# Zero multiplications ahead of 61 TensorE operations, in the operation's own PSUM bank

## The chip, the cores and the metric

The kernel runs on one core of a Trainium2 chip. The metric is the time of one execution on the device in microseconds (us); lower is better. Times of the kernel before are given as the median of three executions. Everything else is read from one further execution that the hardware profiler recorded.

The engines are named as in the profile: PE is TensorE (PEld its weight loads), DVE is VectorE, ACT is ScalarE, POOL is GpSimd, SP is the engine that only issues DMAs here.

## The reference, cut to what matters

One layer of a "metaformer" over `x` of shape (8, 128, 128, 96), batch × height × width × channels: a filter in the frequency domain whose weights depend on the input, then a two-layer MLP in emulated low precision, both with residuals.

```python
# B, H, W, C = 8, 128, 128, 96;  MED = 192
x_pre = soa(einsum('bhwc,mc->bhwm', layernorm(x), w1))      # soa(t) = scale * relu(t)**2 + bias
xf    = rfft2(x_pre)                                        # over height and width
r     = softmax(fc2 @ soa(fc1 @ [mean(x), mean(relu(sp_w x))]))   # 3 rates per image and channel
comb  = sum_s r[s] * resized_filter[s]                      # complex, 128 x 65 x 192
x     = x + w2 @ irfft2(xf * comb)

t = layernorm(x)                                            # per token, 96 channels
h = relu(q16(q16(q8(t) @ q8(W1)) + q8(b1)))                 # q8: fp8 e5m2, q16: fp16
x = x + q16(q16(q8(h) @ q8(W2)) + q8(b2))                   # hidden width 384
```

## The kernel before, in words

The Fourier transforms are matrix products with cosine and sine tables, so nearly all of the arithmetic is on PE. For each of the 8 images there are three streams of work, named by a letter and the image number.

- Stream `a` (`before`): 32 steps of four image columns. `scale` on DVE makes the normalised tile `zT` from `xT` and the broadcast reciprocal deviations `rB`; `project` on PE (L672) multiplies it by `W1S`, one PSUM bank for each half (`i0` is 0 or 2); `rectify` and `square` on ACT follow; `transform` on PE (L701) transforms along the height; `put` on ACT (L708) moves it out and `store_y` writes it to DRAM. After the last step the chain `rate_v0`, `rate_p0`, ... `rate_n` computes the softmax over the three filters: `p` steps on PE (L757, L765, L766, L780), `v` steps on DVE (L753, L774, L775), `rate_e` on ACT.
- Stream `s` (`spectrum`): 33 groups of four frequency rows. `along_w` on PE (L874) transforms along the width; `filters_of` (L887) makes the filters; `copy_sr` (ACT) and two `make` (DVE, L913) read the `along_w` banks; DVE and POOL multiply by the filter; every second group `mix_low` and `mix` (L971, L984, L995) multiply by `w2` and `invert` (L1011) transforms back along the height. `rate_n` must be done before the filters are weighed.
- Stream `c` (`after`): 32 steps. `last` (L1123) finishes the inverse transform, `residual` on DVE (L1131) reads it; `measure`, `rstd` and `quantise` normalise; `turn` (key `turn8`, L1156) transposes on PE and `turned` (L1166, DVE) reads it; `first` (L1170) makes three hidden blocks, `accumulated` (L1177, ACT) and `biased` (L1181, DVE) follow, `hidden` (L1185, ACT) makes the fp8 tile `h8`; `second` (L1192) multiplies by `W2q`; `put` (L1203, ACT), `bias` (DVE), `add_up` (L1210, POOL) and `store` end it.

Streams overlap: stream `s` of an image runs beside `a` of the next and `c` of the one before. The first part of the execution has stream `a` of image 0 alone, the last part stream `c` of image 7 alone.

The order is written out by hand. Every operation has a planned time (`STREAMS`, `O`, `OWN`); `in_order` sorts the operations by it, respecting their needs, and hands out six PSUM banks: an operation gets its banks when they come free in that order. The result is one fixed list, emitted in that order; at the end each engine's instructions are tied into that order, so every engine, PE included, works through its list strictly first to last. A bank is a tile of a pool with one buffer for each tag:

```python
def bank(name):
    t = ps.tile([128, 512], F32, name=name, tag=f"bank{free_banks.pop(0)}")
    return t
```

so the first write of an operation into its bank waits until the last reader of the bank's previous tile has finished. That reader is on ACT or DVE. `zeros` is a constant bf16 tile of 128 × 64 zeros that `mix_low` already multiplies by to clear its banks. Semaphores are placed by the framework.

## Time and profile before

| | |
|---|---|
| median of three executions | 2752.43 us (2752.04 to 2754.02) |
| profiled execution, span from first to last instruction | 2754.4 us |
| PE busy | 2567.8 us, 93% of the span, 25130 matmuls and as many weight loads |
| DVE, ACT, POOL busy | 83%, 81%, 77% |
| mean granted PE clock | 0.970 of full speed |
| DMA | 618.05 MB, mean 224 GB/s |

The profiled execution's own time is its span; the page gives nothing around it. It is 0.07% above the median of the three. "Granted clock" is the share of its full clock that the throttle allowed PE at that time. A group's idle time is that of its engine just before its instructions, and the name behind the arrow is what ended the wait.

### The profile page before, as it was taken

Reading aid. Unit: us, or ns where it says so; the run is one execution under the profiler, and the core shown is the slowest. Engines: PE = TensorE matmul, PEld = TensorE weight load, DVE = VectorE, ACT = ScalarE, POOL = GpSimd, SP = SyncE. Lnnn points to the kernel's source line nnn. Section 1 sums busy time; section 2 is a strip of 40 time slices with the busy share of each in tenths; the row PEclk is TensorE's granted clock in tenths of the full one; section 3 lists DMA queues with packets and bytes.
Section 4 is the critical chain, followed back from the end, with each engine's and each line's share of the span. In section 5 each row is a group of like instructions: output and inputs, shape, how many; then the busy total and the mean of one; then the engine's idle time right before and its main releaser. Section 6 shows DMA issues by size and latency. Waiting matters only on the chain.

```text
span 2754.4 us, 69406 instructions
## 1 busy us (share of the span) xinstructions
PE 2567.8 (93%) x25130; PEld 1953.0 (71%) x25130; DVE 2276.1 (83%) x5887; ACT 2233.0 (81%) x4452; POOL 2122.2 (77%) x3246
## 2 busy tenths in 40 slices
PE   4989999999999999999999999999999998999765
PEld 2668877777677777777677777777777776677433
DVE  3557667798898999889898889889889878999786
ACT  2665556699888879889998878889988997888898
POOL 1239997888788878988688969888788886889432
PEclk9899999999999999999999999999999998999896
DMA  7888777977688866878687757888777774656441
GB/s 205 263 263 253 242 224 241 287 233 251 209 255 260 252 213 196 271 242 262 220 258 245 243 171 220 273 259 257 231 239 242 230 222 147 185 178 190 149 129 62
DMA packets 480023, 618.05 MB, mean 224 GB/s; under 512 B 174542, under 2 KB 381270, under 8 KB 479658
## 3 DMA queue, kind: packets, MB, share of 16 engines
q1 hardware_dynamic: 424386, 462.60, 56.8%
q10 hardware_dynamic: 55296, 151.02, 14.7%
q8 instruction: 199, 3.26, 0.5%
q14 instruction: 142, 1.16, 0.1%
HBM read 405.36 MB, written 208.16 MB: 223 GB/s over the span
## 4 chain that ended last, share of the span: by engine, by line
PE 68%; DVE 13%; ACT 7%; POOL 4%; DMA 4%; issue 3%; SPq 1%; POOLq 0%; ACTq 0%; DVEq 0%
PE px L672 13%; PE pz L874 10%; PE py L701 10%; PE pv L995 7%; PE pf L887 6%; PE pg L1011 5%; PE ph L1170 4%; PE pk L1123 4%; PE po L1192 3%; PE pv L984 3%; DVE t L916 3%; DVE y L1181 2%; ACT h L1185 2%; ACT y L1177 2%; DVE st L581 2%
## 5 line engine op out<-in xcount | busy, mean ns | idle before, releaser
L923 POOL TENSOR_TENSOR rr<-t,t 128x390 f32<-128x390 f32 x512 | 520.4, 1017 | 60.4 <-DVE t L916 60.0
L672 PE MATMUL px<-W1S,zT 97*128 97x240 f32 x2048 | 519.4, 379 | 34.1 <-DVE zT L659 29.2
L1177 ACT CAST y<-ph 128x512 f16<-128x512 f32 x768 | 456.0, 603 | 24.2 <-PE ph L1170 22.4
L672 PEld LDWEIGHTS px<-W1S,zT 97*128 97x128 f32 x2048 | 377.2, 194 | 130.0 <-issue 33.7
L1151 ACT ACTIVATE z<-t,ln_m,ln_r 128x96 fp8e5<-128x96 f32 x960 | 461.2, 492 | 8.6 <-POOL ln_m L614 5.7
L1181 DVE TENSOR_SCALAR y<-y,b1q 128x512 f16<-128x512 f16 x768 | 427.5, 568 | 28.2 <-ACT y L1177 25.6
L683 ACT ACTIVATE rl<-px 128x480 f32<-128x480 f32 x512 | 295.7, 581 | 177.5 <-PE px L672 160.2
L701 PE MATMUL py<-X,F 128*128 128x384 f32 x1024 | 430.7, 507 | 2.1 <-ACT X L690 1.9
L1185 ACT ACTIVATE h<-y 128x1536 fp8e5<-128x1536 f16 x256 | 386.2, 1509 | 2.2 <-DVE y L1181 1.6
L659 DVE SCALAR_TENSOR_TENSOR zT<-xT,rB 96x512 f32<-96x512 f32 x256 | 339.8, 1328 | 53.1 <-DMA rB<-Rd 26.5
L874 PEld LDWEIGHTS pz<-F,yt 128*128 128x128 f32 x2080 | 301.4, 192 | 72.0 <-DVE t L1131 5.9
L1210 POOL TENSOR_TENSOR t<-t,o 128x1536 f32<-128x1536 f32 x64 | 210.1, 3282 | 167.8 <-DVE o L1207 165.8
L874 PE MATMUL pz<-F,yt 128*128 128x130 f32 x2080 | 329.0, 281 | 10.2 <-DVE t L1131 4.7
L857 POOL TENSOR_TENSOR tb<-tb,r 128x384 f32<-128x384 f32 (+1 forms) x264 | 287.0, 1087 | 59.7 <-DVE r L808 23.1
L916 DVE TENSOR_TENSOR t<-dm,pf 128x390 f32<-128x390 f32 x512 | 282.6, 552 | 43.8 <-PE pf L887 18.4
L1170 PE MATMUL ph<-zT,W1q 96*128 96x512 fp8e5 x768 | 293.5, 397 | 19.1 <-DVE zT L1166 13.9
L708 ACT COPY yst<-py 128x384 f32<-128x384 f32 x512 | 246.4, 486 | 74.3 <-PE py L701 67.8
L916 DVE TENSOR_TENSOR t<-dp,pf 128x390 f32<-128x390 f32 x512 | 280.3, 548 | 0.0
L940 POOL TENSOR_TENSOR xf<-rr 128x378 f32<-128x378 f32 x256 | 255.3, 997 | 19.7
L995 PEld LDWEIGHTS pv<-w2A,xf 128*128 128x128 f32 x2048 | 246.8, 194 | 13.6 <-issue 1.5
L995 PE MATMUL pv<-w2A,xf 128*128 128x96 f32 x2048 | 255.2, 278 | 0.0
L938 POOL TENSOR_TENSOR xf<-rr 128x390 f32<-128x390 f32 x256 | 250.1, 977 | 0.0
(126 smaller groups left out, 5210.5 us busy)
## 6 DMA issues: line engine op xcount, KB each, us to landing
Yd<-yst ACTq DMA_DIRECT2D x256, 384.0 KB
yt<-Yd SPq DMA_DIRECT2D x256, 384.0 KB
xb<-in_x SPq DMA_DIRECT2D x64, 768.0 KB
xT<-in_xT SPq DMA_DIRECT2D x128, 384.0 KB
rB<-Rd SPq DMA_DIRECT2D x128, 384.0 KB
tb<-T SPq DMA_DIRECT2D x256, 192.0 KB
Vd<-gst ACTq DMA_DIRECT2D x128, 384.0 KB
xr<-in_x SPq DMA_DIRECT2D x64, 768.0 KB
```

The costliest lines, as they stand in the source:

```text
L659: nc.vector.scalar_tensor_tensor(zTs[(b * NU + u) % NZT][:C, :, :], kept["xT", hb][:, :, w].rearrange("c h w -> c w h"), 1.0, kept["rB", h ...
L672: nc.tensor.matmul(px[:, i * (MED + SCTX) : (i + 1) * (MED + SCTX)], lhsT=zTs[(b * NU + u) % NZT][:, i0 + i, :], rhs=W1S, start=True, stop ...
L701: nc.tensor.matmul(py, lhsT=F1, rhs=kept["X", u][:, i0 : i0 + 2, :].rearrange("h w m -> h (w m)"), start=True, stop=True)
L874: nc.tensor.matmul(pz[:, u * 2 * L : (u + 1) * 2 * L], lhsT=y, rhs=F2[:, cs, :], start=True, stop=True)
L916: nc.vector.tensor_tensor(work(name, g), kept[d, g], pair(g, sign, c), ALU.mult)
L923: nc.gpsimd.tensor_tensor(kept["rr", g][:, :, 2 * i : 2 * i + 2, :], kept[ta, g], kept[tb, g][:, :, ::-1, :], op)
L995: nc.tensor.matmul(kept["pv", p, r][:, i * C : (i + 1) * C], lhsT=kept["xf", g][:, cs, r, :], rhs=w2A, start=False, stop=(i == len(_column ...
L1151: nc.scalar.activation(z, t, AF.Identity, bias=m, scale=r, saturate=False)
L1170: nc.tensor.matmul(kept["ph", u, n], lhsT=W1q[:, n * 128 : (n + 1) * 128], rhs=kept["zT", u], start=True, stop=True)
L1177: nc.scalar.copy(kept["y", u][:, n, :], kept.pop(("ph", u, n)))
L1181: nc.vector.tensor_scalar(y, y, b1q[:, n : n + 1], 0.0, ALU.add, ALU.max)
L1185: nc.scalar.activation(kept["h8", u], kept["y", u], AF.Copy, saturate=False)
```

## The change

A table `WARM` lists, for 61 operations of PE, a number between 1 and 24; the numbers add up to 340. Before such an operation is emitted, `keep_warm` takes a tile in the first of the banks that the operation is about to use and emits that many matmuls into its first 64 partitions: `zeros` as weights (128 rows × 64 columns), and one column of `zeros` repeated 512 times as the moving operand. Each is a complete product of its own (`start` and `stop`), nobody reads it, and the operation then takes its own tile in the same bank. Nothing else is added, removed or moved: no DMA, no instruction of another engine, and the order of the old instructions is the same on every engine.

```diff
+WARM = {
+    ('a', 0): {('project', 0, 2): 24, ('project', 4, 2): 4, ('project', 6, 2): 6, ('project', 8, 2): 7, ('project', 16, 2): 9, ('project', 24, 2): 9, ('project', 28, 2): 5},
+    ('a', 1): {('transform', 1, 2): 4, ('project', 3, 0): 7, ('rate_p2',): 5},
+    ('a', 2): {('rate_p0',): 9},
+    ('a', 3): {('project', 3, 0): 4, ('rate_p2',): 10},
+    ('s', 3): {('along_w', 0, 0): 6},
+    ('c', 2): {('second', 19): 6, ('first', 21, 0): 5},
+    ('a', 5): {('rate_p2',): 9},
+    ('c', 3): {('second', 14): 3},
+    ('s', 4): {('mix_low', 12): 4},
+    ('a', 6): {('project', 0, 0): 5},
+    ('a', 7): {('project', 3, 0): 6, ('rate_p2',): 7},
+    ('s', 6): {('along_w', 0, 1): 2, ('invert', 13, 1): 22},
+    ('c', 5): {('turn8', 4, 3): 4, ('first', 24, 0): 5, ('first', 25, 0): 6},
+    ('s', 7): {('along_w', 9, 0): 3, ('along_w', 13, 1): 12, ('invert', 14, 0): 5},
+    ('c', 6): {('turn8', 6, 3): 2, ('second', 24): 2, ('first', 27, 0): 11, ('first', 29, 0): 8, ('first', 30, 0): 6},
+    ('c', 7): {('turn8', 0, 0): 16, ('first', 1, 0): 3, ('second', 1): 4, ('second', 2): 4, ('second', 3): 4, ('second', 4): 1, ('second', 5): 4, ('second', 6): 4, ('second', 7): 4, ('second', 8): 1, ('second', 9): 4, ('second', 10): 2, ('second', 13): 4, ('second', 15): 4, ('second', 16): 1, ('second', 17): 4, ('second', 19): 4, ('second', 20): 1, ('second', 21): 4, ('second', 23): 4, ('second', 24): 1, ('second', 25): 3, ('second', 26): 3, ('second', 27): 3, ('second', 30): 4, ('second', 31): 7},
+}
...
+    def keep_warm(op):
+
+        n = WARM.get(op.key[0], {}).get(op.key[1:], 0)
+        if n:
+            t = ps.tile([128, 512], F32, name="warm", tag=f"bank{free_banks[0]}")
+            for _ in range(n):
+                nc.tensor.matmul(t[:64, :], lhsT=zeros, rhs=zeros[:, :1].to_broadcast([128, 512]), start=True, stop=True)
...
     for op, banks in in_order(ops):
         free_banks[:] = banks
+        keep_warm(op)
         op.what(*op.args)
```

## The prediction

> **What bounds the kernel now.** I read the page first, then the chain of waits, [...] then the timeline at every place that the table names.

> ```profile
> span 2754.4 us, 69406 instructions
> ...
> PE 2567.8 (93%) x25130; PEld 1953.0 (71%) x25130; DVE 2276.1 (83%) x5887; ACT 2233.0 (81%) x4452; POOL 2122.2 (77%) x3246
> ...
> PE   4989999999999999999999999999999998999765
> ...
> PEclk9899999999999999999999999999999998999896
> ...
> PE 68%; DVE 13%; ACT 7%; POOL 4%; DMA 4%; issue 3%; SPq 1%; POOLq 0%; ACTq 0%; DVEq 0%
> ```

> PE is busy in nearly every slice from the third to the 33rd, and holds 68% of the chain. So a us of PE time saved or lost in the middle should mostly reach the end. In the last 150 us PE has idle time; there ACT is nearly full.

> The clock is not lost evenly. Stretches (start:end, length, then busy us and count of PE, PEld, DVE, ACT, POOL; then PE clock, DMA share, GB/s) [...]:

> ```profile
> 699.80:703.20 3.40, 1.55 (x17) 1.18 (x18) 3.37 (x12) 0.91 (x3) 3.32 (x5) 1.00 1.01 306
> 703.20:706.60 3.40, 3.40 (x9) 2.07 (x8) 1.03 (x2) 1.86 (x5) 3.15 (x8) 0.51 0.38 123
> ...
> 2645.40:2648.80 3.40, 2.24 (x18) 1.29 (x18) 3.02 (x8) 1.84 (x5) 3.23 (x6) 1.00 0.79 248
> 2648.80:2652.20 3.40, 1.38 (x17) 1.02 (x18) 2.81 (x10) 3.31 (x7) 1.59 (x8) 1.00 1.21 323
> 2280.20:2283.60 3.40, 1.47 (x39) 1.20 (x31) 3.30 (x13) 1.03 (x3) 3.31 (x6) 1.00 0.42 157
> 2283.60:2290.40 6.80, 6.80 (x36) 6.30 (x35) 4.01 (x10) 1.40 (x4) 2.73 (x5) 0.50 1.06 285
> ```

> [...] half-clock stretches are 3.4, 6.8 or 10.2 us, apart from the last. [...]

> **The price of one.** The nearest row is `first`, 512 moving columns with its own weight load.

> ```profile
> 2314.10 0.60 PE L1170 MATMUL ph<-zT,W1q 96*128 96x512 fp8e5 x2
> ...
> 2726.52 1.05 PE L1170 MATMUL ph<-zT,W1q 96*128 96x512 fp8e5 x2
> 2727.89 0.63 PE L1170 MATMUL ph<-zT,W1q 96*128 96x512 fp8e5 x1
> ```

> One takes 0.38 us at full clock (1035.74 in the timeline), two take 0.60: 0.22 us for each further one. At half clock 1.05 − 0.63 = 0.42. The 340 cost 340 × 0.22 = 75 us of PE time warm. Their weight loads lie beside the preceding product (a load of 128 columns of fp8 is about 0.10 us).

> **Where they cost nothing.** At 51 places the bank had been read out before PE went idle, and PE waited for an operand. There n × 0.22 is 0.4 to 0.8 of the wait, for instance:

> ```profile
> 701.65 0.25 PE L757 MATMUL pm<-ones,s 128*48 128x1 f32 x2 [2.59 <-DVE s L753]
> ...
> 2283.09 1.81 PE L780 MATMUL pl<-fc2T,hrep 36*128 36x192 f32 x6 [1.93 <-DVE hrep L775]
> ```

> 9 × 0.22 = 1.98 in 2.59 us, 7 × 0.22 = 1.54 in 1.93 us. They end 0.1 to 0.8 us before the operand comes, so the wait covers them. At half clock the cover is gone: 7 × 0.42 = 2.9. The framework could also make the operation wait for its last zero product to complete; one alone takes 0.38, so that is 0 to 0.16 us for each place, inside the same spare; I take 0.

> **Where they delay.** At ten places the wait was for the bank itself, so the zero products can begin only when the operation itself could, and everything behind it on PE's fixed list is later by all of them:

> ```profile
> 2301.84 0.55 DVE L913 TENSOR_TENSOR dm<-pz,sr 128x390 f32<-128x390 f32 x1
> ...
> 2302.53 1.62 PE L1011 MATMUL pg<-V,GL 128*128 128x384 f32 x2 [6.26 <-DVE dm L913]
> ```

> The 6.26 us before `invert 13` end when DVE's `make` has read the bank of `along_w 30`. Its 22 products then start at 2302.4 and take 22 × 0.22 = 4.8 us of full-speed PE time; behind them wait 30 us of PE work that is the chain itself. The ten, in us at full speed: `along_w` of s3 1.3, `mix_low 12` 0.9, `along_w` of s6 0.4, `invert 13` 4.8, `along_w 9` of s7 0.7, `along_w 13` of s7 2.6, `invert 14` 1.1: 11.8 on the chain. `turn8` of c5 (0.9) stands before PE's own 6 us of idleness, and the two of c6 (0.4 each) where ACT carries the chain: 0. Upper end, if the zeros run at half clock and don't raise it: 19.

> **What is gained.** What a half-clock stretch costs is half of the chain's PE time in it, since PE work doubles there:

> ```profile
> 2284.91 3.66 PE pv L995 x16
> ...
> 2311.94 1.81 PE pv L995 x16
> ```

> I added up the chain's PE pieces inside each half-clock stretch of the middle: from 423.4 us 6.8, 703.2 3.4, 1024.1 6.0, 1624.8 2.8, 1635.1 6.5, 1699.9 3.4, 2000.3 3.4, 2283.6 6.3; together 38.6. (In that from 1362.0 DVE has the chain: 0.) All but 1699.9 follow a wait that the table fills; filled, their windows come to 2.2 us busy and more. So (38.6 − 3.4)/2 = 17.6. PE then meets DVE (44 to 47 of each 50 us busy) sooner, so I let 85% through: 15.0; bounds 5 and 17.6.

> Stream a of image 0 has 22.9 us of the chain's PE time at half clock (78.6 to 85.4, 112.7 to 122.9, 181 to 184, 191 to 195), at most 11.4 to gain. But its chain alternates with DMAs (rB, xT, Yd), and a PE that arrives sooner waits longer for them, perhaps long enough to cool again. I take 45%: 5.1; bounds 0 and 11.4. The 24 before `project 0` gain nothing: from 30.5 they end by about 38, and the operand comes at 42.8, [...].

> The stops from 2297.3 and 2413.3 remain, as nothing can run before the bank is free. From 2566 on ACT or a POOL–ACT loop holds the chain. What is left to gain is `second 31`, 1.14 us cold against 0.68, and two small ones before it: 0.7; bounds −2 to +1 (its 7 products take 2.9 us cold in a wait of 1.95).

> **Sum.** −15.0 − 5.1 + 11.8 × 0.85 (10.0) − 0.7 = −10.8 us. Against the span of 2754.4 that is 2743.6. The median is 2.0 below that span, so 2741.6: **2742**.

> **Rivals.**
> (1) Zero products don't count as activity. [...] Then nothing is gained, and the delays stand at 11.8 to 19, cold: about 2766. Slower.
> (2) They count, but DVE and ACT, at 83% and 81% with their own fixed lists, take the chain over. For: the chain from 2333 to 2413 alternates between DVE and PE. Against: 280 us stretches with PE full. At 30% let through and nothing in image 0: −5.3 + 11.8 − 0.7, about 2758. It decides from the point where, without image 0's part, less than 0.63 of the 17.6 gets through: then the change is a loss, and below 0.32 one of over 0.2%.
> (3) Gains and delays cancel: 60% let through, nothing in image 0: −10.6 + 10.0 − 0.7, about 2751.

> **Chances.** Forecast 0.49, (1) 0.15, (2) 0.15, (3) 0.21. A difference under 0.2% (5.5 us) can't be told from none here. Faster 0.49, within 0.21, slower 0.30. Best case −17.6 − 11.4 + 8 − 1 = −22. The range, 2730 to 2762, runs from just inside it to the middle of the slow cases; the forecast's own range is 2730 to 2747.

> **What would show it.** Right: half-clock stretches of the middle gone but near 1700; `invert 13` later by 4 to 5 us behind its 22; the clock from 423 to 2284 above 0.99. Wrong: half clock right behind a filled wait (rival 1), or a clear middle whose span from 423 to 2284 is not some 12 us shorter (rival 2). Zero products at 0.42 us in the filled waits would break the cover.

## The result, and the profile after

| | before | after |
|---|---|---|
| median, 21 executions each | 2753.02 us (2744.46 to 2763.03) | 2750.03 us (2740.78 to 2757.69) |
| ratio after to before | | 0.9986, 95% interval 0.9977 to 0.9995 |
| profiled execution, span | 2754.4 us | 2739.0 us |
| mean granted PE clock in it | 0.970 | 0.990 |

The change is 0.14% faster, about 3.9 us (0.0014 × 2753). That is real but under the 0.2% that I had set as telling; I had forecast 10.8. The value lies in the whole range of 2730 to 2762, which takes in the rivals, but outside the 2730 to 2747 that belonged to the forecast itself.

The two profiles differ by 15.4 us, the medians by 3. An execution's time is 1.8 us above its span, which I had taken for one and the same before. So the profiled execution of after (2740.78) was the fastest of its 21, and that of before (about 2756) was 3 us above its median. Single executions of one kernel differ by over 10 us here, so a difference of two profiles is no measure of this change. It can still be read place by place.

From the page of after, the lines that answer to those shown of before: span, busy time, PE's and its clock's slices, the chain.

```profile
span 2739.0 us, 70084 instructions
...
PE 2608.2 (95%) x25470; PEld 1955.4 (71%) x25470; DVE 2276.7 (83%) x5887; ACT 2230.2 (81%) x4452; POOL 2123.6 (78%) x3246
...
PE   6999999999999999999999999999999998999876
...
PEclk9999999999999999999999999999999999999998
...
PE 70%; DVE 10%; ACT 8%; POOL 4%; DMA 4%; issue 3%; SPq 1%; POOLq 0%; ACTq 0%; DVEq 0%
```

There are 340 more matmuls and 340 more weight loads, and no other engine has one instruction more or less. The clock is at 90% or more in every slice but the last. Now stretches of 3.40 and 6.80 us around the same two waits as before, `rate_p0` of image 2 and `rate_p2` of image 7 (columns as in the prediction):

```profile
687.16:690.56 3.40, 2.80 (x23) 1.65 (x22) 3.37 (x12) 0.85 (x3) 3.32 (x6) 1.00 1.00 294
690.56:693.96 3.40, 3.40 (x21) 2.48 (x21) 1.72 (x5) 2.82 (x7) 3.15 (x7) 1.00 0.36 124
2258.50:2261.90 3.40, 3.03 (x42) 1.84 (x35) 3.30 (x13) 0.97 (x3) 3.31 (x6) 1.00 0.46 163
2261.90:2268.70 6.80, 6.80 (x75) 5.65 (x74) 3.95 (x10) 4.29 (x8) 2.66 (x4) 1.00 1.02 280
```

Before, the stretches at these waits held 1.55 and 1.47 us of PE work, and a granted clock of 0.51 and 0.50 followed. Now they hold 2.80 and 3.03, and 1.00 follows. In the 6.8 us behind `rate_p2` PE ran 75 matmuls in place of 36.

These stretches are laid around the waits. Where the clock itself changed can be read off the traces: in those of before and after it is 1.00 or 0.50 throughout, and its 49 changes before and 21 after lie whole multiples of 3.413 us apart in each, to within 0.003 us. Cut into stretches of 3.413 us at those points, the trace of after has the two waits mostly in 685.0 to 688.4 and 2258.6 to 2262.0: 1.29 and 1.41 us of PE work without the products, 3.37 and 3.04 with them, and full clock in the next. In the five profiles with the middle filled, 46 stretches cut in the same way between 415 and 2270 us hold at most 2.03 us of other PE work and some products beside it; all but one (1.45 us with its products) are followed by full clock, among them all 11 of the trace of after (1.82 us and more with theirs). In the trace of before, from 48 us on, where its record of the clock begins, every such stretch at full clock with less than 1.78 us of PE work was followed by half clock, and those with 1.78 to 2.03 went either way.

The timeline of the same places, PE alone:

```profile
686.26 2.15 PE L430 MATMUL warm<-zeros 128*64 128x512 bf16 x9
689.01 0.22 PE L784 MATMUL pm<-ones,s 128*48 128x1 f32 x2 [0.60 <-DVE s L780]
...
2259.34 1.71 PE L430 MATMUL warm<-zeros 128*64 128x512 bf16 x7
2261.42 1.21 PE L807 MATMUL pl<-fc2T,hrep 36*128 36x192 f32 x6 [0.37 <-DVE hrep L802]
```

The operations still wait 0.60 and 0.37 us for their operand when the products have ended, close to what had been worked out (0.61 and 0.39). The bank wait, from the chain of waits in order of time:

```profile
2277.20 0.48 DVE dm L940
2277.72 7.27 PE warm L430 x22
2285.04 0.91 PE pg L1038 x2
```

The 22 products stand on the chain itself, 7.3 us long, the first 4.7 us at half clock (which lasts from 2275.6 to 2282.4). In the trace of before `invert` itself began at half clock (1.62 us for its first two matmuls, from 2302.53, against 0.91 here), so the whole 7.3 are not the loss.

To see where time went I subtracted the start of each PE operation in the profile of before from that of the same operation after. This **shift** was −11.0 us at 212 us, stayed there to the digit up to 414, fell in steps at the filled waits to −21.8 at 2232, rose to −16.4 at 2436 behind the bank waits, and ended at −15.4. So there are four parts: the start, the middle, the bank waits and the end. The experiments measure each alone.

### The profile page after: what moved, and what is told of

Its sections match the earlier page's. It is cut to its first block, busy times and chain, and to the rows that moved or that the text cites. A ratio compares the mean times of both kernels' runs of the same rounds, so it can differ in the third digit from the quotient of the medians.

```text
span 2739.0 us, 70084 instructions
## 1 busy us (share of the span) xinstructions
PE 2608.2 (95%) x25470; PEld 1955.4 (71%) x25470; DVE 2276.7 (83%) x5887; ACT 2230.2 (81%) x4452; POOL 2123.6 (78%) x3246
## 3 DMA queue, kind: packets, MB, share of 16 engines
q8 instruction: 202, 3.31, 0.5%
## 4 chain that ended last, share of the span: by engine, by line
PE 70%; DVE 10%; ACT 8%; POOL 4%; DMA 4%; issue 3%; SPq 1%; POOLq 0%; ACTq 0%; DVEq 0%
PE px L699 13%; PE pz L901 11%; PE py L728 10%; PE pv L1022 8%; PE pf L914 6%; PE pg L1038 5%; PE ph L1197 4%; PE pk L1150 4%; PE po L1219 3%; PE pv L1011 3%; ACT y L1204 2%; ACT h L1212 2%; DVE t L943 2%; DVE y L1208 2%; POOL t L1237 2%
## 5 line engine op out<-in xcount | busy, mean ns | idle before, releaser
L699 PE MATMUL px<-W1S,zT 97*128 97x240 f32 x2048 | 510.5, 374 | 15.0 <-DVE zT L686 13.1
L699 PEld LDWEIGHTS px<-W1S,zT 97*128 97x128 f32 x2048 | 370.7, 191 | 105.9 <-issue 15.0
L728 PE MATMUL py<-X,F 128*128 128x384 f32 x1024 | 422.7, 499 | 1.6 <-DVE dm L940 0.8
L1197 PE MATMUL ph<-zT,W1q 96*128 96x512 fp8e5 x768 | 286.9, 388 | 11.6 <-DVE zT L1193 8.0
```

Source lines behind the costliest of these rows:

```text
L699: nc.tensor.matmul(px[:, i * (MED + SCTX) : (i + 1) * (MED + SCTX)], lhsT=zTs[(b * NU + u) % NZT][:, i0 + i, :], rhs=W1S, start=True, stop ...
L728: nc.tensor.matmul(py, lhsT=F1, rhs=kept["X", u][:, i0 : i0 + 2, :].rearrange("h w m -> h (w m)"), start=True, stop=True)
L1197: nc.tensor.matmul(kept["ph", u, n], lhsT=W1q[:, n * 128 : (n + 1) * 128], rhs=kept["zT", u], start=True, stop=True)
```

## The experiments

All but the two repeats are the changed kernel with another `WARM`, and all are compared with the kernel before on the same chip.

**The changed kernel and the kernel before, again.** No edit.

> The changed kernel once more, for a second profile. In the first profile its span was 15.4 us under that of the profile of before, while the medians of many executions differ by 3.0. Theory A ([...] in most executions some filled wait still ends in half clock): the second profile has a span of 2745 to 2752, shows more half clock than the first (0.984 to 0.988 mean), and the shift against before is lost in a few steps of 1.5 to 3 us at half-clock stretches. Theory B (the first profile was an outlier in the DMA-fed start of image 0, where it gained 11 us): mean clock in the middle as in the first profile, and the shift at 200 us is -5 or less in size instead of -11, the rest alike.

> The kernel before once more, for a second profile: how far do two profiled executions of the same kernel lie apart, and where? Theory A: half-clock stretches of 3.4 us appear and vanish at waits of 1 to 2 us between the two, spans differ by several us. Theory B: they differ mostly before 200 us, in the DMA-fed start.

Measured: after again 0.9974 (0.9961 to 0.9987), span 2741.9; before again 1.0001 (0.9989 to 1.0014), span 2752.9. The shift of after again was −9.2 at 212 us, −19.9 at 2232 and −14.6 at 2436: the steps in the middle and behind the bank waits repeat. Neither theory holds as I put it: the second profile gained 9 us in the start too, and lost nothing in the middle. That profiled execution was again the fastest of its set (2743.69, the lowest of 11), which the median is not.

**Without the ten bank waits**, and **the ten bank waits alone**. The edit of the first is shown; the second keeps just what it takes out.

```diff
-    ('s', 3): {('along_w', 0, 0): 6},
-    ('s', 4): {('mix_low', 12): 4},
-    ('s', 6): {('along_w', 0, 1): 2, ('invert', 13, 1): 22},
...
```

> Only the 51 places whose bank was already read out; the ten whose wait is for the bank are left out (278 products). If the ten delays cost what the first profile shows (the shift went from -21.7 at 2283 us to -15.4 at 2413 us, 6.3 us) this is 5 to 10 us faster than the whole change: about 2741 to 2745, ratio 0.995 to 0.997 to before. If the delays are given back by the engines behind PE, it equals the whole change, ratio 0.9986.

> Only the ten places whose wait is for the bank (62 products). My sum: 11.8 us on the chain, 85 percent let through, 8 to 12 us slower than before, ratio 1.003 to 1.0045. If the delays are absorbed: 0 to 3 us slower.

Measured: without them 0.9940 (0.9923 to 0.9956), 16.5 us faster, more than I had expected; the ten alone 1.0037 (1.0021 to 1.0052), 10.2 us slower. Put together they leave 6 us faster, between the two measurements of the whole change (3.9 and 7.2). So most of the delay reaches the end, near the price I had put on it (10.0).

**The largest of them alone.**

```diff
+    ('s', 6): {('invert', 13, 1): 22},
```

> Only the 22 products ahead of invert 13 of image 6, whose wait is for the bank. By my sum 22 x 0.22 = 4.8 us on the chain, ratio 1.0015 to 1.002. In the profile of the ten bank places the shift rose by 5.6 us from 2273 to 2354 us. If it is absorbed behind it: ratio 1.000 to 1.0005.

Measured: 1.0021 (1.0012 to 1.0031), 5.8 us slower. Its profile's shift rose from 6.4 at 2273 us to 11.7 at 2603. Little of the 22 is absorbed behind it.

**The middle alone**, eleven places from `rate_p2` of image 1 to `rate_p2` of image 7.

```diff
-    ('a', 0): {('project', 0, 2): 24, ...
-    ('a', 1): {('transform', 1, 2): 4, ('project', 3, 0): 7, ('rate_p2',): 5},
+    ('a', 1): {('rate_p2',): 5},
...
-    ('s', 3): {('along_w', 0, 0): 6},
-    ('s', 4): {('mix_low', 12): 4},
-    ('s', 6): {...},
-    ('c', 5): {...},
-    ('s', 7): {...},
-    ('c', 6): {...},
-    ('c', 7): {...},
```

> Only the eleven places between 415 and 2290 us whose bank was free (69 products). From the shifts of three profiles against before: between 212 and 2232 us they fell by 10.8, 10.6 and 10.9 us, then 2.6 more at the last softmax. So 11 to 14 us faster, ratio 0.995 to 0.996, with no half clock between 415 and 2290 but behind a place that is not in the table. If the other engines took the chain over (my second rival), 5 us, ratio 0.998.

Measured: 0.9957 (0.9943 to 0.9972), 11.8 us faster. Half clock between 415 and 2290 is left at 731 us, behind a wait of 1.48 us at `filters_of`, which isn't in the table, and from 2284, inside the bank wait of `invert 13`, which is not filled here. In us the interval is 7.7 to 15.7 (0.0028 and 0.0057 × 2753): my 15.0 lies in it, my second rival's 5.3 does not. So the other engines did not take the chain over to the extent that this rival had.

**One product at each of these places** in place of 3 to 10.

```diff
-    ('a', 1): {('rate_p2',): 5},
-    ('a', 2): {('rate_p0',): 9},
+    ('a', 1): {('rate_p2',): 1},
+    ('a', 2): {('rate_p0',): 1},
...
```

> The same eleven places of the middle, one product each instead of 3 to 10. [...] the half-clock stretches near 420, 700, 1022, 1360, 1625, 1998 and 2282 us stay, and the time is that of before, within 3 us. If any activity inside the wait were enough, it equals the kernel with all 69: 11 to 14 us faster.

Measured: 0.9977 (0.9967 to 0.9987), 6.3 us faster (3.6 to 9.1): between the two expectations, about half of the full table's gain with 11 products for 69, though the two intervals touch. A product that stands alone keeps PE busy for 0.40 us in this trace, not 0.22. Half clock between 415 and 2270 us adds up to 24 us there, against 31 to 51 in the seven profiles with no product in that stretch, and 3 in that with all eleven places filled. The stretch near 1360 us, which all eight profiles without a filled wait there show, is missing; those near 417, 697, 1022, 1619, 1629 and 1991 us remain. So one product was enough at some of these places and not at others, in this one profile.

**The start alone**, and **the start with three more places**.

```diff
+    ('a', 0): {..., ('project', 12, 2): 8, ('project', 20, 2): 5},
+    ('a', 1): {..., ('project', 4, 0): 5},
```

> Only the nine places of the start, where image 0's stream a has PE alone with its DMAs (75 products). My prediction let 45 percent of 11.4 us through: 5.1 us, ratio 0.998. Theory A (the waits of the start move from one step to another between executions, as rB lands, so a fixed table fills waits of one execution and misses those of others): a gain of 0 to 3 us in the median, ratio 0.999 to 1.000, and the profile shows a PE wait over 2 us at a step without products, with half clock behind it. Theory B (the start gains what the first profile showed, 11 us): ratio 0.996, and the loss is elsewhere.

> The nine places of the start and three more where other executions had their waits: project 12 (8 products), project 20 (5) and project 4 of image 1 (5). Ten profiles show PE's waits over 1 us either at steps 8, 16, 24 or at 12, 20, 24, 28. If only the moving of the waits kept the start from gaining, covering both sets gives 3 to 6 us, ratio 0.998 to 0.999. If the DMAs hold the start and PE only waits longer, nothing: ratio 0.9994 as with nine places, or 1 to 2 us slower by the 13 products of 2.9 us in all that some executions don't cover.

Measured: the nine places 0.9994 (0.9985 to 1.0004); with twelve 0.9983 (0.9974 to 0.9992), 4.7 us faster. The waits do move. In six of the eight profiles that had no products in the start PE waited over 1 us at step 16, near 111 us; in those of the ten bank places and of the end alone it did so at step 12, near 95 us, and not at 16. In the profile without the bank waits, whose start is that of the change, `rB` landed late for step 12, which the table leaves out. Its timeline, then its stretches:

```profile
93.06 1.07 DVE L682 SCALAR_TENSOR_TENSOR zT<-xT,rB 96x512 f32<-96x512 f32 x1 [6.34 <-DMA rB<-Rd]
...
94.20 1.97 PE L695 MATMUL px<-W1S,zT 97*128 97x240 f32 x8 [3.39 <-DVE zT L682]
```

```profile
96.30:103.10 6.80, 6.80 (x16) 4.17 (x17) 4.63 (x16) 2.85 (x5) 1.21 (x5) 0.53 0.84 272
```

A wait of 3.39 us, and 6.8 us of half clock with PE full. In the profile of the start alone a wait of 2.92 us at `project 4` of image 1 was followed by half clock in the same way (a mean granted clock of 0.52 from 193.9 to 197.3): the wait ahead of step 3 had been filled, and PE waited at the next step in its place. With five products there too, in the profile of twelve places, 2.78 us of that wait remain and half clock follows all the same (191.3 to 198.1); it is the last wait over 1 us but that ahead of step 0. The intervals of nine and twelve places overlap between 0.9985 and 0.9992, so that the three more help is likely and not proved.

A wait that has moved away also leaves its products behind as work. The chain of the start alone, in order of time, at step 16:

```profile
107.77 1.29 PE py L714 x4
109.06 2.09 PE warm L416 x9
```

In the profile without the bank waits such products hold 4.7 us of the chain in the start, in those of the change none.

**The end alone**, 31 places after 2330 us, and **the end with at most two products ahead of each `second`** of image 7.

```diff
-    ('c', 7): {..., ('second', 1): 4, ('second', 2): 4, ('second', 3): 4, ...
+    ('c', 7): {..., ('second', 1): 2, ('second', 2): 2, ('second', 3): 2, ...
```

> Only the 31 places after 2330 us whose bank was free (134 products), most of them in stream c of image 7. I expected 0.7 us: ACT and a POOL-ACT loop hold the chain there, so the clock rises and the time doesn't: ratio 0.999 to 1.0005. If PE's half speed mattered there, up to 4 us, ratio 0.9985.

> The 31 places of the end, but at most 2 products ahead of each second of image 7 instead of up to 7. In the profile with all of them, four products that began at half clock took 1.92 us in a wait of 1.3 and second 21 came 0.9 us later. Two take 1.05 us even at half clock. If that overflow is the 2.8 us that the 134 products cost, this one is within 1 us of before, ratio 0.9996 to 1.0004. If it is something else in the end, it stays near 1.001.

Measured: the end alone 1.0010 (1.0001 to 1.0019), 2.8 us slower though the clock rose to 0.979, just beyond what I had expected; with at most two 0.9999 (0.9988 to 1.0009). The timelines of PE, first with up to four, then with two:

```profile
2699.32 1.92 PE L417 MATMUL warm<-zeros 128*64 128x512 bf16 x4
2701.29 0.99 PE L1206 MATMUL po<-W2q,h 128*128 128x96 fp8e5 x12
```

```profile
2702.86 0.62 PE L417 MATMUL warm<-zeros 128*64 128x512 bf16 x2
2704.23 1.06 PE L1206 MATMUL po<-W2q,h 128*128 128x96 fp8e5 x12 [0.75 <-ACT h L1199]
```

and ACT in the first of the two kernels:

```profile
2698.86 1.48 ACT L1199 ACTIVATE h<-y 128x1536 fp8e5<-128x1536 f16 x1
```

Both show `second 21` and the products ahead of it. ACT's `h` was there at 2700.34 (2698.86 + 1.48), but the four products, begun at half clock, took 1.92 us, and `second 21` started at 2701.29: 0.95 us late. With two products the operation still waits 0.75 us for `h`, as it should. `second 21` itself is not on the chain of that profile, but overflows like it are, at `first 1` and `second 17` (chain of waits, end alone):

```profile
2603.67 1.43 PE warm L417 x3
...
2681.27 1.57 PE warm L417 x4
2682.85 0.04 issue
2682.89 1.13 PE po L1206 x12
```

With at most two the chain holds no zero product in the end; the three ahead of `first 1`, the same in both kernels, ran at full clock there (a granted clock of 1.00 from 2608.8 us). The shift from 2603 to 2740 us rises by 2.3 us in the end alone and 1.0 to 1.2 in the three other profiles with that table, and falls by 0.1 with at most two; in the other eight it moves by −0.4 to 0.7. So the overflow is the likeliest cause of the 2.8 us; the intervals of the two kernels overlap between 1.0001 and 1.0009, so the difference itself is at the limit of what the runs can tell. Nor did the end gain from the clock: between 2330 and 2740 us half clock sums to 41 us with the end filled, 67 before and 65 to 94 in the other profiles with nothing there, and still nothing is won. That fits the chain, which the prediction read as ACT's or a POOL–ACT loop's from 2566 on.

**The middle and the twelve places of the start**, 162 products, none at a bank wait or in the end.

```diff
+    ('a', 0): {..., ('project', 12, 2): 8, ('project', 20, 2): 5},
+    ('a', 1): {..., ('project', 4, 0): 5},
-    ('s', 3): {('along_w', 0, 0): 6},
-    ('s', 4): {('mix_low', 12): 4},
-    ('s', 6): {...},
-    ('c', 5): {...},
-    ('s', 7): {...},
-    ('c', 6): {...},
-    ('c', 7): {...},
```

> The eleven free-bank places of the middle and the twelve of the start (162 products), none ahead of a bank wait and none in the end. If the parts add: 0.9957 and 0.9983 to before make 0.994, 15 to 17 us faster, about 2739 to 2741. If the start's gain is lost again later (the streams behind it fed by DMA at their own pace): as the middle alone, 0.9957.

Measured: 0.9953 (0.9934 to 0.9972), median 2741.22 in six executions (2740.2 to 2744.8). It is some 13 us (0.0047 × 2753) faster than the kernel before. Its interval lies apart from that of the change's first comparison (0.9977 to 0.9995) and overlaps that of the second (0.9961 to 0.9987). What the start adds to the middle is not shown: 13 against 11.8 alone, with ±5 and ±4. Nor is it shown to be better than the table without its ten bank waits (0.9940 with 51 places): their intervals overlap from 0.9934 to 0.9956. Its page:

```profile
span 2739.7 us, 69728 instructions
...
PEclk9999999999999999999999999999999999999886
...
PE 65%; DVE 13%; ACT 7%; POOL 7%; DMA 4%; issue 3%; SPq 1%; POOLq 0%; ACTq 0%; DVEq 0%
```

The clock of the last slices is lower than in the change, where it is at 9 nearly throughout, and its mean is 0.978 against 0.990: yet the kernel gains more over before. So does the table without its ten bank waits, with 0.985, and its interval lies below both of the change's. So the mean granted clock does not rank these kernels. Half clock in the middle, where the prediction found PE on the chain, went from 31 to 51 us to 3 with its places filled, and 11.8 us were gained; in the end, where it found ACT or a POOL–ACT loop, it went from 67 to 41, and nothing was.

## Why the prediction was right or wrong

Two terms of the forecast's sum failed. The start was to give 5.1 us, 45% of what half clock cost there, and gave 1.7. The end was to give 0.7 and cost 2.8. The forecasts for the middle and the bank waits lie inside the measured intervals.

| part | predicted, us | measured alone, us (95%) |
|---|---|---|
| middle | −15.0 | −11.8 (−15.7 to −7.7) |
| bank waits | +10.0 | +10.2 (+5.8 to +14.3) |
| start | −5.1 | −1.7 (−4.1 to +1.1) |
| end | −0.7 | +2.8 (+0.3 to +5.2) |
| sum, and the whole measured | −10.8 | −0.5; whole −3.9 and −7.2 |

The parts add up to −0.5 us with some ±7 (their half-intervals, 4, 4, 3 and 2.5, added as squares), which takes in the whole. The forecast's 10.8 us are 6.9 too many by the first comparison, 3.6 by the second. The two failed terms make up 3.4 + 3.5 = 6.9; with ±3 on each, that they match so exactly is luck, and a middle weaker than 15.0 may have its share. The three free parts alone sum to −10.7, and together (51 places) measured −16.5 (−21.2 to −12.1); with ±5 on that sum they can be the same, so whether the parts help each other stays open.

- **That zeros count as activity: right here.** The forecast assumed it; no row of before had shown it. Stretches that the products alone raised from 1.29 and 1.41 us of PE work to 3.37 and 3.04 are followed by full clock (1.00), and the middle gains 11.8 us. Rival 1 falls.
- **Half of the chain's PE time in the half-clock stretches, 85% let through: held.** The interval takes in 15.0 and excludes rival 2. That 11.8 is the better number for the let-through (67% of 17.6) can't be claimed.
- **Bank waits: right in mechanism; the size in part by luck.** Priced at 4.8, `invert 13` alone measured 5.8 (3.3 to 8.5). The seven places that I had put on the chain are the ones that stand there in the profile of after, but with 16.5 us in place of 11.8, as the products ahead of `invert 13` (7.3) and `along_w 13` (4.0) ran in part at half clock. That the ten still cost 10.2 means that some of this would have been slow without them, or is absorbed; the runs do not tell which.
- **Start: the 45% let-through was mis-sized.** Its 5.1 us lie outside the interval; 1.7 of 11.4 are 15%. I had named the right danger, that a PE arriving sooner waits longer for the DMAs and falls to half clock again, but had taken the waits of one execution as given places. The profiles show that they move between steps, in the one shown with the landing of `rB`, so a fixed table misses some, and products whose wait has moved stand on the chain (2.1 us in the profile of the start alone).
- **End: the term with the wrong sign.** Predicted −0.7, it measured +2.8. The bound of +1 came from `second 31` alone. I had written that at half clock the cover is gone and did not carry it to the two dozen other `second`s, where waits of about 1.3 us stand beside four products at 0.42 each, with the clock still falling there about every 17 us (half clock from about 2647, 2664, 2681 and 2698 us in the profile of the end alone). That overflow stands on the chain at `second 17`; that it is the whole loss is likely, not shown.
- **The outcome of rival 3, not its reason.** Its 2751 lies nearest to the result, by 60% let through in the middle and nothing at the start. That fits the start better than my 45%, and 10.6 lies in the middle's interval; what it did not have is the loss in the end.
- **What I had asked of the trace came**: half-clock stretches of the middle are gone (415 to 2270 us at full clock), `invert 13` is later (by more than its 4 to 5 us: the shift rises by 7.0 from 2290 to 2303), the clock from 423 to 2284 is above 0.99, and products in the filled waits ran at 0.22.

That the middle's 12 us and the bank waits' 10 nearly cancel makes a large change end in a small result, and the forecast had this: the gain is real and is given back later, at places where the same products can only be work. What it did not have is that the start and the end add so little.

## What to carry to other kernels

Fill a wait only where the bank is already free and the operand is what is late; where the bank is the wait, every product is added to PE's own list, here at nearly its full price (10.2 us measured for the 11.8 worked out). Count the fill at the price measured at half clock (0.42 us a product, not 0.22), since it is needed just where the clock may have dropped, and put it at waits that several profiles show at the same operation: where the wait has moved, the fill is work too. Time the parts of such a change separately: the whole here is the small difference of +10 and −12.

## What was not expected of the hardware

Here an operation waits until its last zero product has completed, which I had bounded at 0.16 us, as something that the framework could do, and taken at nothing. In the timeline of after, at a bank wait (`along_w 0` of s3):

```profile
1020.40 1.46 PE L430 MATMUL warm<-zeros 128*64 128x512 bf16 x6 [1.89 <-ACT yst L735]
...
1021.92 0.52 PEld L901 LDWEIGHTS pz<-F,yt 128*128 128x128 f32 x4 [0.54 <-PE warm L430]
1021.92 0.71 PE L901 MATMUL pz<-F,yt 128*128 128x130 f32 x4
```

Six products at 0.22 would be 1.32 us; the operation starts after 1.52, and its weight load waits for `warm` by name. That is 5 × 0.22 + 0.38 for the last, and 0.04. If each such place costs 0.2 us more as this one does, that is some 1.4 us by estimate at the seven bank waits on the chain, which fits the +10.2 without being told apart in it.

And one product, 0.40 us, at each of eleven waits gave 6.3 us (3.6 to 9.1), about half the gain of 69 (11.8, 7.7 to 15.7).
